# Graph-attention layer with a leading-row search on one Trainium2 core: another load order, another drain, and stores of one block

## The chip, the cores and the metric

The kernel runs on one core of one Trainium2 chip. A core has five engines, each with an instruction stream of its own, which it works off in order: TensorE (PE in the profile; its weight loads are PEld), VectorE (DVE), ScalarE (ACT), GpSimd (POOL) and SyncE (SP). Here SP only issues DMAs, GpSimd issues the indirect ones, and ScalarE issues a few. Matmuls write PSUM, the other engines work on PSUM and SBUF, and 16 DMA engines move data between SBUF and HBM. The metric is the device time of one execution in microseconds (us), lower is better.

## The reference

One graph-attention layer with a residual and a layer norm. x is 4096 x 512, adj is 4096 x 4096 and stands for additive masks, W is 512 x 2048 (four heads of 512), all float32:

```python
ht = (h @ W).reshape(N, N_HEADS, N_HIDDEN).transpose(1, 0, 2)
src = jnp.einsum('hnd,hd->hn', ht, a_src)
dst = jnp.einsum('hnd,hd->hn', ht, a_dst)
e = jax.nn.leaky_relu(src[:, :, None] + dst[:, None, :], SLOPE) + adj_mat[None]
att = jax.nn.softmax(e, axis=-1)
h_prime = jnp.einsum('hij,hjd->hid', att, ht)
return h_prime.mean(axis=0)
...
x = _layernorm(x + _L0_gnn_ref(x, adj, L0_gnn_W, L0_gnn_a), axis=-1)
```

The entries of adj reach 1e9, so in nearly every row one entry leads the others by so much that the softmax is 1 at that column and 0 elsewhere, for every head. Then the layer's output in that row is the row of x at the leading column, times the mean of the four heads of W.

## The kernel before, in words

`leading_rows` (line 66) computes every row that way and also tests whether that was allowed; `general` (line 389) computes the full attention for the row blocks where it was not. The test's result is one number, `any_bad`, which the engines load at line 60 to skip `general`; with these inputs it is skipped.

The 4096 rows are 32 blocks of 128, one row to a partition, and row p of block ib is row 32p + ib of the matrix. Per block:

- `load_adj` (101) brings 128 x 4096 numbers of adj, 2 MB, in one DMA on the SP queue (four DMAs for the first and the last block). There are six buffers, and a load is issued five blocks ahead.
- `segment_maxima` (146): VectorE takes the largest of each of 64 segments of 64 numbers, in two reductions of half a row (four pieces for the first and last block). `find_segment` (159) takes the eight largest segment maxima (`top`) and their places, and GpSimd gathers the leading segment of each row again from HBM (`lead`, 256 B a row).
- `find_column` (173), two blocks later: the largest in the segment (`inner`), its place, and so the column; GpSimd then gathers that row of x (`y`, 2 KB a row).
- `project` (189), three blocks later: TensorE turns y by four transposes into PSUM (`tp`, line 201), ScalarE copies that to SBUF (`yt`, line 203), and TensorE adds in PSUM the residual, as a matmul of the block of x with the identity (line 194), and four matmuls of yt with `w_sum`, the mean of the heads (line 209). A float32 matmul shows in the trace as two instructions.
- `stats` (215), `rstd` (222) and `finish` (227): mean and variance on ScalarE, the square root on ScalarE with a reciprocal and a product on VectorE, for two blocks at a time, and the normalised block written by ScalarE into `hold`. `hold` has a place of 512 numbers per partition for each of the 32 blocks. It first holds x, and W in places 16 to 31, and at the end the output.

W comes as four blocks of 1 MB (`load_w`, 111), and x as eight groups of four blocks (`load_x`, 108). `mean_of_heads` (245) adds the four heads of one W block on TensorE. `turn_w` and `head_vector` turn W for the vectors that the test's bound needs, spread over t = 1 to 14, and `bound` runs at t = 28 to 30.

The order of the work is written out by hand: each engine runs its instructions in the order in which the program names them. The loop at line 334 runs t over the 32 blocks. In the order of lines 335 to 366 it issues loads, half of the maxima of block t, the column of block t - 2, the other half, the segment of block t, the projection of block t - 3, statistics of block t - 4, and every second t the finishes of blocks t - 6 and t - 5.

The drain starts at line 368 when the loop is over: columns of blocks 30 and 31, finishes of 26 and 27, stores of blocks 0 to 27 in seven DMAs of four blocks (8 KB in a run), the test (309), whose count over the partitions is a small matmul (320) and three small operations of VectorE, and then projections of 29, 30 and 31, each followed by statistics and finish of the block before it. `finish_last` (231) normalises block 31 on VectorE with its batch-norm instructions, and ScalarE's queue stores it.

A DMA on the SP queue waits on SP for its buffer or its data, and everything behind it on that queue waits too.

Of the kernel before, what the change touches and what calls it, by code (L numbers as in the profile page):

```python
# [9 lines left out]
F32 = mybir.dt.float32  # L10
U32 = mybir.dt.uint32
# [8 lines left out]
P = 128  # L20
# [45 lines left out]
def leading_rows(ctx, tc, x, adj, W, a, out, ident, v, n_bad, any_bad):  # L66
# [7 lines left out]
    nc = tc.nc  # L74
# [4 lines left out]
    Q = 4  # L79
# [31 lines left out]
    def load_w(kb):  # L111
        nc.sync.dma_start(hold[:, ds(w_at + kb * H, H), :], w_blocks[:, kb])

    load_adj(0)
    for s in range(2):
        nc.scalar.dma_start(a_rows[ts(s, H), :], a[:, ts(s, D), :].rearrange("h d o -> h (d o)"))
    load_w(0)
    load_w(1)
    load_adj(1)
    load_w(2)  # L120
    load_w(3)
    load_adj(2)
    load_x(0)
    for ib in range(3, AHEAD):
        load_adj(ib)

    make_identity(nc, ident)
# [15 lines left out]

    seg_of, at_of, lead_of, y_t, o_ps = {}, {}, {}, {}, {}

    def segment_maxima(ib, part):

        if part == 0:
            seg_of[ib] = small.tile([P, S], F32, name="seg")
        n = PIECES if ib in (0, NB - 1) else 2  # L150
        for k in range(part * n // 2, (part + 1) * n // 2):
            nc.vector.tensor_reduce(  # L152
                seg_of[ib][:, ts(k, S // n)],
                adj_t[ib][:, ts(k, N // n)].rearrange("p (s e) -> p s e", e=E), axis=AX.X, op=OP.max,
            )
        if part == 1:
            del adj_t[ib]

    def find_segment(ib):
        seg = seg_of.pop(ib)  # L160
# [9 lines left out]
        )  # L170
        at_of[ib], lead_of[ib] = at, lead

    def find_column(ib):
        lead = lead_of.pop(ib)
        nc.vector.max(out=inner[:, ib, :], in_=lead)  # L175
        within = small.tile([P, 8], U32, name="within")
        nc.vector.max_index(within, inner[:, ib, :], lead)  # L177
        col = small.tile([P, 1], U32, name="col")
        nc.vector.scalar_tensor_tensor(  # L179
            col, at_of.pop(ib)[:, 0:1], float(E), within[:, 0:1], op0=OP.mult, op1=OP.add  # L180
        )
        y = rows.tile([P, D], F32, name="y", bufs=4)
        nc.gpsimd.indirect_dma_start(  # L183
            out=y, out_offset=None, in_=x,
            in_offset=bass.IndirectOffsetOnAxis(ap=col[:, :1], axis=0),
        )
        y_t[ib] = y

    def project(ib, between=(), wait=False):

        o = o_ps[ib] = psum.tile([P, D], F32, name="o")

        def residual():
            nc.tensor.matmul(o, ident, hold[:, ib, :], start=True, stop=False)  # L194

        if wait:
            residual()
        y = y_t.pop(ib)
        tp = psum.tile([P, KB, P], F32, name="tp", bufs=2)
        for kb in range(KB):  # L200
            nc.tensor.transpose(tp[:, kb, :], y[:, ts(kb, P)], ident)  # L201
        yt = rows.tile([P, KB, P], F32, name="yt")
        nc.scalar.copy(yt, tp)  # L203
        if not wait:
            residual()
        for some in between:
            head_vector(*some)
        for kb in range(KB):
            nc.tensor.matmul(o, yt[:, kb, :], w_sum[:, kb, :], start=False, stop=(kb == KB - 1))  # L209

    def row_norm(ib):
        sq = rows.tile([P, D], F32, name="sq")
# [15 lines left out]
        i = slice(ib, ib + 1)  # L228
        nc.scalar.activation(hold[:, ib, :], o_ps.pop(ib), AF.Identity, bias=nm[:, i], scale=sd[:, i])  # L229

    def finish_last(ib):
        o = o_ps.pop(ib)
        st = small.tile([P, nc.vector.BN_STATS_DIM], F32, name="st", bufs=1)
        nc.vector.bn_stats(st, o)
        mv = small.tile([P, nc.vector.BN_AGGR_DIM], F32, name="mv", bufs=1)
        nc.vector.bn_aggr(mv, st)
        r = small.tile([P, 1], F32, name="r", bufs=1)
        nc.scalar.activation(r, mv[:, 1:2], AF.Sqrt, bias=eps)
        nc.vector.reciprocal(r, r)
        nc.vector.tensor_scalar(hold[:, ib, :], o, mv[:, 0:1], r, op0=OP.subtract, op1=OP.mult)  # L240
# [52 lines left out]
    def bound(part):  # L293
# [11 lines left out]
        else:  # L305
            nc.vector.tensor_mul(lead_by, of_bound[1], vn)
            nc.vector.tensor_scalar(lead_by, lead_by, 1.05, 110.0, op0=OP.mult, op1=OP.add)

    def test():
        a1 = top[:, :, 0]  # L310
        gap = once.tile([P, NB], F32, name="gap")
        nc.vector.tensor_tensor(gap, top[:, :, 1], inner[:, :, 1], op=OP.max)
        size = once.tile([P, NB], F32, name="size")
        nc.vector.scalar_tensor_tensor(size, a1, -1.0, a1, op0=OP.mult, op1=OP.max)
        nc.vector.tensor_sub(gap, a1, gap)
        nc.vector.tensor_scalar(size, size, -(2.0 ** -22), lead_by, op0=OP.mult, op1=OP.subtract)
        nc.vector.scalar_tensor_tensor(gap, gap, 0.9999, size, op0=OP.mult, op1=OP.add)
        nc.vector.tensor_scalar(gap, gap, 0.0, None, op0=OP.is_gt)
        pg = psum.tile([1, NB], F32, name="px", bufs=1)
        nc.tensor.matmul(pg, ones[:, 0:1], gap, start=True, stop=True)  # L320
        nc.vector.tensor_scalar(n_bad, pg, -1.0, float(P), op0=OP.mult, op1=OP.add)
        total = once.tile([1, 1], F32, name="total")
        nc.vector.tensor_reduce(total, pg, axis=AX.X, op=OP.add)
        nc.vector.tensor_scalar(any_bad, total, -1.0, float(N), op0=OP.mult, op1=OP.add)
# [9 lines left out]
    for t in range(NB):  # L334
        if t in x_at:
            load_x(x_at[t])
        load_adj(t + AHEAD)
        segment_maxima(t, 0)
        if t >= COLUMN:
            find_column(t - COLUMN)  # L340
        segment_maxima(t, 1)
        find_segment(t)
        pair = t >= FINISH and t % 2 == 0
        if pair:
            rstd(slice(t - FINISH, t - FINISH + 2))
        if t == 0:
            for kb in range(KB):
                mean_of_heads(kb)
            turn_a()
        turned = [(*vectors[0], turn_w(*vectors.pop(0))) for _ in range(vectors_at.get(t, 0))]  # L350
        if t == 16:
            head_norms()
        if 28 <= t <= 30:
            bound(t - 28)
        if t >= PROJECT:
            project(t - PROJECT, turned)
        else:
            for some in turned:
                head_vector(*some)
        if pair:  # L360
            finish(t - FINISH)
            finish(t - FINISH + 1)
        if t >= STATS:
            stats(t - STATS)
        for ib in norms_at.get(t, ()):
            row_norm(ib)

    find_column(NB - 2)
    find_column(NB - 1)
    rstd(slice(NB - FINISH, NB - FINISH + 2))  # L370
    finish(NB - FINISH)
    finish(NB - FINISH + 1)
    for g in range(NB // Q - 1):
        store(nc.sync, g * Q, Q)
    test()
    for ib in range(NB - PROJECT, NB):
        project(ib, wait=(ib == NB - 1))
        stats(ib - 1)
        rstd(slice(ib - 1, ib))
        finish(ib - 1)  # L380
        if ib == NB - 2:
            store(nc.sync, NB - Q, 2)
    store(nc.sync, NB - 2, 1)
    finish_last(NB - 1)
    store(nc.scalar, NB - 1, 1)


# [232 lines left out]
```

## Time and profile before

| what | value |
|---|---|
| time, median of 6 runs | 256.96 us (256.31 to 258.1) |
| the profiled execution | 258.13 us, of which the span of the program's instructions is 256.4 us |
| busy share of the span | TensorE 80%, VectorE 75%, ScalarE 47%, GpSimd 24% |
| moved by DMA | 97.75 MB, mean 381 GB/s |
| VectorE's reductions (line 152) | 68, 146.2 us busy |
| TensorE's matmuls with w_sum (line 209) | 256, 119.6 us busy, 610 ns mean |
| TensorE's residuals (line 194) | 64, 36.3 us busy, 652 ns mean |
| adjacency loads, 2 MB each | 32.6 us from issue to landing (median) |
| gathers of x | 8.2 us from issue to landing (median) |
| stores of four blocks, 1 MB each | 25.9 us from issue to landing (median) |

The page of the profile shows one execution. Its rows of digits cut the span into 40 slices of 6.4 us, where a digit is the busy share in tenths (PEclk is the clock granted to TensorE, in tenths of full speed). A line of the timeline gives start and duration in us, the engine, the line of the program and the operation, then output and inputs by the program's names, and in brackets how long the engine had been idle and what released it. A "q" behind an engine's name is its instruction sequencer, which issues DMAs.

### The profile page before, as it was taken

How to read it: one execution, taken by the hardware profiler on the slowest of the kernel's cores; microseconds unless marked ns; L12 is line 12 of the kernel's file. 1: busy time of each engine (PE TensorE's matmuls, PEld its weight loads, DVE VectorE, ACT ScalarE, POOL GpSimd, SP SyncE). 2: the span in 40 equal slices, each digit the busy share in tenths (PEclk: the TensorE clock that was granted, in tenths of full speed). 3: DMA queues.
4: the chain of work that ended last, by engine and by line, in shares of the span. 5: the costliest groups of instructions: out<-in, count | busy, mean ns of one | idle time of the engine just before them, and what ended most of it. 6: DMA issues, size and time to landing. Idle time of an engine off the chain costs nothing.

```text
span 256.4 us, 2438 instructions
## 1 busy us (share of the span) xinstructions
PE 205.8 (80%) x683; PEld 104.9 (41%) x684; DVE 191.9 (75%) x381; ACT 120.3 (47%) x295; POOL 61.8 (24%) x75
## 2 busy tenths in 40 slices
PE   0099995999898999998595978888785989929960
PEld 0033584655554556653242424333332434404420
DVE  3508379969979997997989999999799999721011
ACT  2000322357645475755272537575655555615450
POOL 1100022222222322232212332323223222310000
PEclk9999965999999999999999799999999799986997
DMA  7999999999999999999999999999999999975021
GB/s 247 410 422 435 422 425 422 414 424 430 418 421 421 422 427 419 425 414 422 424 422 422 422 419 420 423 432 417 417 421 428 414 404 425 426 299 206 35 91 50
DMA packets 12259, 97.75 MB, mean 381 GB/s; under 512 B 1992, under 2 KB 1992, under 8 KB 5968
## 3 DMA queue, kind: packets, MB, share of 16 engines
q1 hardware_dynamic: 8496, 87.82, 82.0%
q0 software_dynamic: 3584, 9.44, 9.5%
q10 hardware_dynamic: 160, 0.28, 0.3%
q8 instruction: 7, 0.11, 0.2%
q14 instruction: 12, 0.10, 0.1%
HBM read 89.15 MB, written 8.39 MB: 380 GB/s over the span
## 4 chain that ended last, share of the span: by engine, by line
DMA 59%; DVE 27%; PE 9%; issue 2%; ACT 0%; POOLq 0%; SPq 0%
DMA adj_t<-in_adj_dram 41%; DVE seg L152 20%; DMA hold<-in_L_gnn_W_dram 7%; PE o L209 6%; DMA y<-in_x_dram,col 6%; DMA lead<-in_adj_dram,row 6%; PE o L194 2%; DVE within L177 1%; DVE at L163 1%; PE tp L201 1%; DVE top L161 1%; DVE inner L175 1%; DVE col L179 1%; DVE row L165 1%; DVE hold L240 0%
## 5 line engine op out<-in xcount | busy, mean ns | idle before, releaser
L152 DVE TENSOR_REDUCE seg<-adj_t 128x32 f32<-128x2048 f32 (+1 forms) x68 | 146.2, 2154 | 28.9 <-DMA adj_t<-in_adj_dram 28.8
L209 PE MATMUL o<-w_sum,yt 128*128 128x512 f32 x256 | 119.6, 610 | 0.7 <-ACT yt L203 0.7
L209 PEld LDWEIGHTS o<-w_sum,yt 128*128 128x128 f32 x256 | 47.5, 195 | 61.5 <-issue 48.7
L183 POOL DMA_INDIRECT y<-in_x_dram,col x32 | 30.2, 945 | 97.9 <-issue 79.8
L167 POOL DMA_INDIRECT lead<-in_adj_dram,row x32 | 30.3, 948 | 70.7 <-DVE row L165 47.4
L203 ACT COPY yt<-tp 128x512 f32<-128x512 f32 x32 | 18.8, 586 | 52.0 <-PE tp L201 43.0
L201 PE MATMUL tp<-ident,y 128*128 128x128 f32 x128 | 21.3, 292 | 20.1 <-DMA y<-in_x_dram,col 20.1
L194 PE MATMUL o<-hold,ident 128*128 128x512 f32 x64 | 36.3, 652 | 0.0
L201 PEld LDWEIGHTS tp<-ident,y 128*128 128x128 f32 x128 | 15.0, 148 | 33.2 <-issue 30.6
L248 PE MATMUL o<-hold,ident 128*128 128x512 f32 x32 | 16.7, 682 | 12.6 <-DMA hold<-in_L_gnn_W_dram 12.6
L229 ACT ACTIVATE hold<-o,nm,sd 128x512 f32<-128x512 f32 x31 | 22.6, 779 | 7.9 <-DVE nm L225 7.9
L266 ACT COPY wt<-tp 128x512 f32<-128x512 f32 x16 | 9.2, 586 | 33.2 <-PE tp L264 30.1
L220 ACT ACTIVATE sq<-o,nm 128x512 f32<-128x512 f32 x31 | 21.3, 687 | 1.0
L272 PEld LDWEIGHTS pv<-at_d,wt 128*128 128x128 f32 x128 | 18.3, 212 | 7.2 <-issue 4.6
L213 ACT ACTIVATE sq<-hold 128x512 f32<-128x512 f32 x32 | 19.8, 619 | 0.0
L218 ACT ACTIVATE sq<-o 128x512 f32<-128x512 f32 x31 | 18.7, 604 | 0.0
L272 PE MATMUL pv<-at_d,wt 128*128 128x2 f32 x128 | 17.1, 258 | 0.5 <-ACT wt L266 0.5
L248 PEld LDWEIGHTS o<-hold,ident 128*128 128x128 f32 x32 | 6.8, 220 | 21.4 <-issue 20.2
L249 ACT ACTIVATE w_sum<-o 128x512 f32<-128x512 f32 x4 | 2.4, 597 | 24.6 <-PE o L248 24.6
L224 DVE RECIPROCAL sd<-sd 128x2 f32<-128x2 f32 (+1 forms) x17 | 2.7, 159 | 14.6 <-ACT sd L223 14.6
L175 DVE MAX8 inner<-lead 128x8 f32<-128x64 f32 x32 | 7.0, 218 | 5.8 <-DMA lead<-in_adj_dram,row 5.8
L194 PEld LDWEIGHTS o<-hold,ident 128*128 128x128 f32 x64 | 10.6, 207 | 0.5 <-issue 0.5
(66 smaller groups left out, 94.8 us busy)
## 6 DMA issues: line engine op xcount, KB each, us to landing
adj_t<-in_adj_dram SPq DMA_DIRECT2D x30, 2048.0 KB, 32.6
hold<-in_x_dram SPq DMA_DIRECT2D x8, 1024.0 KB, 29.5
out_dram<-hold SPq DMA_DIRECT2D x7, 1024.0 KB, 25.9
adj_t<-in_adj_dram SPq DMA_DIRECT2D x8, 512.0 KB, 6.7
hold<-in_L_gnn_W_dram SPq DMA_DIRECT2D x4, 1024.0 KB
lead<-in_adj_dram,row POOLq DMA_INDIRECT x32
y<-in_x_dram,col POOLq DMA_INDIRECT x32, 8.2
out_dram<-hold SPq DMA_DIRECT2D x1, 512.0 KB
```

Of the source, the lines that this page charges most:

```text
L152: nc.vector.tensor_reduce(seg_of[ib][:, ts(k, S // n)], adj_t[ib][:, ts(k, N // n)].rearrange("p (s e) -> p s e", e=E), axis=AX.X, op=OP.max,)
L167: nc.gpsimd.indirect_dma_start(out=lead, out_offset=None, in_=adj_segs, in_offset=bass.IndirectOffsetOnAxis(ap=row[:, :1], axis=0),)
L183: nc.gpsimd.indirect_dma_start(out=y, out_offset=None, in_=x, in_offset=bass.IndirectOffsetOnAxis(ap=col[:, :1], axis=0),)
L194: nc.tensor.matmul(o, ident, hold[:, ib, :], start=True, stop=False)
L201: nc.tensor.transpose(tp[:, kb, :], y[:, ts(kb, P)], ident)
L203: nc.scalar.copy(yt, tp)
L209: nc.tensor.matmul(o, yt[:, kb, :], w_sum[:, kb, :], start=False, stop=(kb == KB - 1))
L213: nc.scalar.activation(sq, hold[:, ib, :], AF.Square, accum_out=xx[:, ib : ib + 1])
L220: nc.scalar.activation(sq, o, AF.Square, bias=nm[:, i], accum_out=sd[:, i])
L229: nc.scalar.activation(hold[:, ib, :], o_ps.pop(ib), AF.Identity, bias=nm[:, i], scale=sd[:, i])
L248: nc.tensor.matmul(o, ident, hold[:, w_at + kb * H + h, :], start=(h == 0), stop=(h == H - 1))
L272: nc.tensor.matmul(pv[:, kb, h : 2 * H : H], wt[:, k, :], at_d[:, k, h : 2 * H : H], start=(k == 0), stop=(k == KB - 1),)
```

## The change

Four things change, and all the other lines stay.

- **Loads.** Before: adj 0, W 0, W 1, adj 1, W 2, W 3, adj 2, x 0, adj 3, adj 4. After: adj 0, W 0, adj 1, W 1, adj 2, W 2, adj 3, W 3, adj 4, x 0. The means of heads follow: block 0 at t = 0, 1 at t = 1, 2 and 3 at t = 2 (before, all four at t = 0).
- **Block 31's maxima.** At t = 31 only the first of four pieces stands ahead of `find_column(29)`, the other three behind it.
- **Drain.** For block 31 the column comes from a search of the whole row of 4096 for its largest value, without the gathered segment; the segment is still gathered, and its `inner` is taken later, for the test. The test is cut in two, and its matmul and three small operations come behind the projection of block 30. Blocks 29 and 30 no longer add the residual on TensorE: `finish_last` adds it on VectorE and normalises these blocks there. Block 31's copy from PSUM is shared by ScalarE and VectorE.
- **Stores.** Blocks 0 to 23 go out in 24 DMAs of one block, with 2 KB in a run, ahead of the finishes of 26 and 27 in program order; then 24 to 27 in one, and 28 to 31 each in one.

```diff
-    load_w(0)
-    load_w(1)
-    load_adj(1)
-    load_w(2)
-    load_w(3)
-    load_adj(2)
+    for kb in range(KB):
+        load_w(kb)
+        load_adj(kb + 1)
     load_x(0)
...
+    def find_inner(ib):
+        nc.vector.max(out=inner[:, ib, :], in_=lead_of[ib])
+
+    def find_column_in_row(ib):
+
+        col = small.tile([P, 8], U32, name="col")
+        nc.vector.max_index(col, top[:, ib, :], adj_t[ib])
+        gather_rows(ib, col)
...
-        nc.scalar.copy(yt, tp)
-        if not wait:
+        if order == "residual turn":
+            half = KB // 2
+            nc.scalar.copy(yt[:, :half, :], tp[:, :half, :])
+            nc.vector.tensor_copy(yt[:, half:, :], tp[:, half:, :])
+        else:
+            nc.scalar.copy(yt, tp)
+        if order == "turn residual":
             residual()
...
-    def finish_last(ib):
+    def finish_last(ib, residual):
+
         o = o_ps.pop(ib)
+        if residual:
+            nc.vector.tensor_add(hold[:, ib, :], o, hold[:, ib, :])
+            o = hold[:, ib, :]
...
     find_column(NB - 2)
-    find_column(NB - 1)
+    find_column_in_row(NB - 1)
     rstd(slice(NB - FINISH, NB - FINISH + 2))
+    for ib in range(NB - 2 * Q):
+        store(nc.sync, ib, 1)
     finish(NB - FINISH)
     finish(NB - FINISH + 1)
-    for g in range(NB // Q - 1):
-        store(nc.sync, g * Q, Q)
+    store(nc.sync, NB - 2 * Q, Q)
+    project(NB - 3, order="turn")
+    find_inner(NB - 1)
     test()
-    for ib in range(NB - PROJECT, NB):
-        project(ib, wait=(ib == NB - 1))
-        stats(ib - 1)
-        rstd(slice(ib - 1, ib))
-        finish(ib - 1)
-        if ib == NB - 2:
-            store(nc.sync, NB - Q, 2)
+    stats(NB - 4)
+    rstd(slice(NB - 4, NB - 3))
+    finish(NB - 4)
+    store(nc.sync, NB - 4, 1)
+    finish_last(NB - 3, True)
+    store(nc.sync, NB - 3, 1)
+    project(NB - 2, order="turn")
+    count()
+    finish_last(NB - 2, True)
     store(nc.sync, NB - 2, 1)
-    finish_last(NB - 1)
+    project(NB - 1, order="residual turn")
+    finish_last(NB - 1, False)
     store(nc.scalar, NB - 1, 1)
```

## The prediction

> **What bounds the kernel now.** I read the forty slices first, then the chain of waits, then the timeline of the last 50 us, and last the stretches of the clock.
>
> ```profile
> PE   0099995999898999998595978888785989929960
> DVE  3508379969979997997989999999799999721011
> PEclk9999965999999999999999799999999799986997
> DMA  7999999999999999999999999999999999975021
> GB/s 247 410 422 435 422 425 422 414 424 430 418 421 421 422 427 419 425 414 422 424 422 422 422 419 420 423 432 417 417 421 428 414 404 425 426 299 206 35 91 50
> ```
>
> A slice is 6.4 us. Up to slice 35 (228 us) the DMA engines are full at 404 to 435 GB/s: 97.75 MB at 422 GB/s are 232 us of the 256.4 us span. Nothing before 228 us can gain unless bytes go, and none go. What can move is the drain, the last 28 us, where the GB/s row falls away. There the timeline shows what ends last:
>
> ```profile
> 228.60 0.23 DVE L175 MAX8 inner<-lead 128x8 f32<-128x64 f32 x1 [5.45 <-DMA lead<-in_adj_dram,row]
> 229.66 1.45 ACT L229 ACTIVATE hold<-o,nm,sd 128x512 f32<-128x512 f32 x2 [5.80 <-DVE nm L225]
> 230.65 0.27 PE L320 MATMUL px<-gap,ones 128*1 128x32 f32 x2 [4.77 <-DVE gap L318]
> 233.46 4.75 PE L209 MATMUL o<-w_sum,yt 128*128 128x512 f32 x8
> 239.34 3.68 PE L209 MATMUL o<-w_sum,yt 128*128 128x512 f32 x8
> 244.99 1.55 PE L209 MATMUL o<-w_sum,yt 128*128 128x512 f32 x3 [0.68 <-ACT yt L203]
> 248.73 0.70 DVE L234 BATCH_NORM_STATS2 st<-o 128x6 f32<-128x512 f32 x1 [1.67 <-PE o L209]
> 249.46 0.18 DVE L236 BATCH_NORM_AGGREGATE mv<-st 128x2 f32<-128x6 f32 x1
> 249.68 0.29 ACT L238 ACTIVATE r<-mv,eps 128x1 f32<-128x1 f32 x1 [1.81 <-DVE mv L236]
> 250.21 0.81 DVE L240 TENSOR_SCALAR hold<-o,mv,r 128x512 f32<-128x512 f32 x1
> 251.05 0.39 ACTq L243 DMA_DIRECT2D out_dram<-hold  x1
> ```
>
> (Columns: start, duration, engine, line, operation; in brackets the idle time and its releaser.) VectorE waits 5.45 us for the last gathered segment. The count of the test (L320) stands ahead of block 29's projection on TensorE, so TensorE idles 4.77 us, then runs blocks 29, 30 and 31 with almost no hole until 248.73. From there 2.32 us lead to the last store, and 5.28 us (251.05 to 256.33) to the end. The idle time has a second price:
>
> ```profile
> 136.78:140.19 3.41, 1.31 (x4) 0.24 (x2) 3.33 (x6) 0.00 (x0) 0.94 (x1) 1.00 1.01 429
> 140.19:143.60 3.41, 2.77 (x7) 1.74 (x8) 3.25 (x9) 1.64 (x3) 0.94 (x1) 0.50 1.02 424
> 225.53:228.94 3.41, 0.35 (x1) 0.00 (x0) 0.31 (x3) 0.00 (x0) 0.00 (x0) 1.00 0.89 369
> 228.94:232.35 3.41, 1.70 (x7) 1.33 (x8) 1.93 (x14) 1.80 (x3) 0.94 (x1) 0.50 0.26 66
> 232.35:235.76 3.41, 3.41 (x5) 1.32 (x4) 0.32 (x2) 2.67 (x7) 0.00 (x0) 0.50 0.90 362
> ```
>
> (Stretch, length, then busy us of TensorE, its weight load, VectorE, ScalarE, GpSimd, then the granted clock, DMA share, GB/s.) After a stretch with 0.35 us of TensorE work the clock is halved for two stretches. Block 29 from its transposes (230.84) to block 30's takes 7.2 us, where block 30 takes 238.04 to 242.86 = 4.8: the half clock cost 2.4 us. Without it this span would have been 254.0.
>
> **The start.** The order of the loads changes, not their bytes. Block 1 comes one W block (1.05 MB, 2.5 us at 422 GB/s) earlier, block 2 two (5 us), and the last W block later by some 10 us. VectorE starts sooner, but the DMA row is full anyway: worth 0. Against it, TensorE gets two means of heads later. At 125 us a gather waited 4.1 us for TensorE, and the rate between 120 and 128 us was still 419 GB/s, since adjacency loads are issued 32.6 us ahead. So the loss too is 0; I allow 0.5 us each way.
>
> **The stores.** 6.3 MB go out as 24 stores in 2 KB runs instead of six in 8 KB. In the trace a 2 KB packet holds a DMA engine 86 ns, an 8 KB one 309 ns, so 3072 packets on 16 engines take 16.5 us, not 14.8: 1.7 us more, ending near 230. On SP 24 issues of 0.33 us are 8 us of a queue that has nothing else from 191.36 on; stores 24 to 27 stand behind them but wait for ScalarE's finish anyway (229.5), and nobody waits for a store before the end. Worth 0. A gather of x (four 4 KB packets an engine, 160 ns each, in turn with store packets) lands 4 x (309 - 86) = 0.9 us sooner; it gains only where a gather is late, and below none is. The Trainium skill, "DMA: Bandwidth & Descriptors", section "Bandwidth", asks for batches of 1 MiB and speaks against 256 KB stores (it measured 138 GB/s at 64 KB, 341 at 1 MB). An estimate from that page, at some 250 GB/s, would put their end at 238 us, still ahead of the final store. No run here shows such a loss; the 86 ns row gives 381 GB/s.
>
> **The search.** Block 31's segments end at 221.7 as now, since the four reductions and one column search are only reordered (block 29's gather goes 1.2 us sooner). Row and top 222.5, block 30's column 223.15. Then VectorE scans 4096 elements. No row shows that. The 64-wide search takes 0.22; the reductions give 2280 - 1215 = 1065 ns for 1024 more elements, 1.04 ns each; so 0.22 + 4032 x 1.04 ns = 4.4 us. The ends are 0.22 (width free) and 8.6 (two passes); I take 4.4, as one value a step is what the nearest wide row does. It ends at 227.7, against 229.35 now: 1.7 us gained. The gather of x behind it lands by 234 and is not needed before 240.
>
> **The queue behind it.** This search now stands ahead of the reciprocal and product for blocks 26 and 27 (0.3 us, to 228.0), which ScalarE's two finishes await (1.45 us, to 229.4), and behind those stands block 29's copy (0.58). TensorE, no longer blocked by the count, turns block 29 once its gather lands (issued at 219.0, 6.8 to 8.2 us on its way, so 226 to 228), and then idles until the copy is there. Its matmuls thus start at 230.0 instead of 233.46.
>
> **The chain from block to block.** Here I see the loss. The finish of 29 is written ahead of 30's projection, so ScalarE's square root for 29 stands ahead of 30's copy. After 29's last matmul come: add of 128x512, not shown (between 0.6, 512 elements at 1.04 ns plus some 0.1, and 0.81, L240; I take 0.70, L234), statistics 0.70, aggregate 0.18, root 0.29, steps between them 0.13: 2.0 us. Then 30's copy, 0.58 + 0.07. TensorE waits 2.65 us where now it had 1.1 us of transposes and residual to do and no hole. After 30's matmuls the count comes in as well (L320 to L324: 230.65 to 231.40, 0.75), then 2.0, then half a copy (0.4; it was 0.58): 3.2 us. The residual of 31 and its transposes (1.3 us) lie beside that.
>
> **The sum at full clock.** 230.0 + 3.7 = 233.7; + 2.65 + 3.7 = 240.05; + 3.2 + 3.7 = 246.95; + 2.32 + 5.28 = 254.55. The profiled run at full clock was 254.0: there block 29's matmuls would start at 232.2, and 14.2 us (one block of 4.8, and 239.34 to 248.73) lie from there to the last matmul, against 16.95 now. So 2.2 us are gained at the front, 2.75 spent on the two waits, and 0.55 lost.
>
> **The clock.** The hole before block 29, 226 to 230 but for its transposes, is nearly as long as now (4.77), so one stretch at half clock is to be expected: 3.4 to 5 us of it, costing 1.7 to 2.5; I take 2.1. Span 256.65, with the 1.73 us that lie around the profiled span (258.13 - 256.4) 258.4. That execution was 1.2 above the median, 256.96; on the median's footing this is 257.2, and 258.4 on its own. I state 257.8, between, because the new waits give the clock two more occasions to fall. The Trainium skill, "TensorE: Matmul & The Clock Gate", section "Why this matters for your kernels", allows holes of up to about 3 us. By that rule the hole of 2.65 us is harmless and the sum stays. The rows above disagree: 1.31 us busy of 3.41, a total idle of 2.1, was enough at 140.19.
>
> **Rivals.** (1) Forecast: the waits behind the finishes eat the gain, clock lost once; 256.6 to 259.2; chance 0.54. (2) Faster: the clock holds, or the search is quicker than 4.4 us. For it: the hole is a microsecond or two shorter. At full clock 254.55 + 1.73 = 256.3, less the 1.2 by which the profile stood over the median, 255.1; with half the search (2.2 us less) and the clock lost once, 257.2 - 2.2 = 255.0. It decides if matmuls of block 29 start before 229 or run in 3.7 us; 0.22. (3) The clock falls a second time, in the waits of 2.65 and 3.2 us: 3.4 us at half clock cost 1.7 more: 259.5 (up to 261); 0.16. (4) The change doesn't do what it says: the small stores delay the gathers, segment 30 reaches VectorE after 222.5 (it had 0.6 us of slack), and everything shifts by as much, 1 to 3 us: 258.8 to 260.8; 0.08.
>
> Measurement tells 0.3% (0.77 us) from no change. Faster than 256.2: rival 2 and a little of 1, 0.22. Within: the low part of 1, 0.27. Slower than 257.7: 0.51. The range takes in most of 2, all of 1 and part of 3 and 4: 255.2 to 260.3.
>
> **What would show it.** Right: DMA full until 229; a search of 4.4 us ending near 227.7; block 29's transposes near 226 and its matmuls near 230; ScalarE's copy of block 30 released by the root, and TensorE idle some 2.6 and 3.2 us between the last three blocks; last matmul at 247 to 250. Wrong: a search far from 4.4 us, copies not held by the root, matmuls of 29 starting with its transposes, or VectorE waiting on a segment at 222.

## The result, and the profile after

The changed kernel takes 260.21 us in the median of 20 runs (258.09 to 261.88), the kernel before 257.23 us in 46 runs beside it (256.01 to 258.18): a ratio of 1.0111, with an interval of 1.0091 to 1.013. It is slower by 1.1%, some 3 us. The forecast was 257.8 within 255.2 to 260.3, slower with a chance of 0.51. So the side held, the range held by 0.09 us, and the likeliest case of it (256.6 to 259.2) did not: 6 of the 20 runs lie in it and 13 at 259.5 or above. A second series of the same kernel, in the first experiment, has a median of 259.28 us, so a difference from the changed kernel is given below as two numbers where the two medians make it differ. A ratio leaves out runs more than 1.5% above the fastest of their kernel, which touches one experiment alone (the start and the stores as before, three runs of twelve).

The profiled execution, 258.1 us with a span of 256.3, is as short as the fastest of the 20; a longer one, 0.8 us above the median, is shown by the first experiment. First three rows of the forty slices of the changed kernel (6.4 us each):

```profile
PE   0279868999999999989498879698785989938760
...
PEclk9999798699999999999979999979999799997996
...
GB/s 253 435 417 435 405 421 424 413 423 426 415 414 417 422 414 418 418 414 419 421 413 423 418 416 414 414 417 418 422 422 410 419 396 400 390 374 330 41 43 50
```

The row of GB/s was to be as before up to slice 35. It is not quite: from the tenth slice on most read 413 to 422 where before they read 417 to 428. That small loss comes back below. The drain in the timeline (columns as before):

```profile
223.83 4.42 DVE L191 FIND_INDEX8 col<-top,adj_t 128x8 uint32<-128x4096 f32 x1
225.95 0.60 PE L206 MATMUL tp<-ident,y 128*128 128x128 f32 x4
228.54 1.45 ACT L242 ACTIVATE hold<-o,nm,sd 128x512 f32<-128x512 f32 x2 [4.45 <-DVE nm L238]
229.88 0.58 ACT L213 COPY yt<-tp 128x512 f32<-128x512 f32 x1
...
237.62 0.29 ACT L255 ACTIVATE r<-mv,eps 128x1 f32<-128x1 f32 x1 [4.23 <-DVE mv L253]
237.82 0.57 ACT L213 COPY yt<-tp 128x512 f32<-128x512 f32 x1
238.44 3.70 PE L219 MATMUL o<-w_sum,yt 128*128 128x512 f32 x8 [2.09 <-ACT yt L213]
244.56 0.35 ACT L210 COPY yt<-tp 128x256 f32<-128x256 f32 x1
244.97 3.70 PE L219 MATMUL o<-w_sum,yt 128*128 128x512 f32 x8 [1.18 <-ACT yt L210]
```

Block 29's transposes are done at 226.55, but its matmuls start at 230.52, because the copy of 229.88 stands behind the finishes of 26 and 27 (228.54), and these behind the search. Block 30's copy (237.82) comes right after the root of block 29's finish (237.62), as the prediction read from the order. The brackets show 2.09 and 1.18 us of idle TensorE. With block 30's transposes (0.6) before the one, and the count, residual and transposes of block 31 before the other, the waits from the last matmul of a block to the first of the next are 2.52 and 2.83 us. In the chain of work that ended last, block 29's matmuls stand as one piece:

```profile
230.52 5.41 PE o L219 x8
```

A block takes 3.7 us at full clock. The clock of the stretches says why this one took 5.41 (stretch, length, busy us of TensorE, its weight load, VectorE, ScalarE, GpSimd, granted clock, DMA share, GB/s):

```profile
227.39:230.80 3.41, 0.28 (x1) 0.29 (x2) 2.43 (x10) 2.26 (x4) 0.95 (x1) 1.00 1.01 374
230.80:234.22 3.42, 3.42 (x5) 1.36 (x5) 0.32 (x2) 2.10 (x6) 0.00 (x0) 0.50 1.03 393
234.22:237.63 3.41, 2.13 (x8) 0.88 (x6) 1.57 (x3) 0.01 (x1) 0.00 (x0) 1.00 0.53 215
```

After a stretch with 0.28 us of matmuls, one stretch at half clock costs 1.7 us. In this execution the wait before block 30 does not lower it again. That is luck: in the first experiment the same wait does.

### The profile page after: what moved, and what is told of

The parts are those of the page before. It is cut to its first block, busy times and chain, and to the rows that moved or that the text cites. A ratio compares the mean times of both kernels' runs of the same rounds, so it can differ in the third digit from the quotient of the medians.

```text
span 256.3 us, 2464 instructions
## 1 busy us (share of the span) xinstructions
PE 205.6 (80%) x679; PEld 104.7 (41%) x680; DVE 200.4 (78%) x387; ACT 114.7 (45%) x285; POOL 62.0 (24%) x75
## 4 chain that ended last, share of the span: by engine, by line
DMA 59%; DVE 27%; PE 5%; issue 4%; ACT 1%; SPq 1%; POOLq 0%
DMA adj_t<-in_adj_dram 55%; DVE seg L149 18%; PE o L219 5%; DMA y<-in_x_dram,col 4%; DVE col L191 2%; DVE within L181 1%; DVE at L158 1%; DVE top L156 1%; DVE st L251 1%; DVE col L183 1%; DVE inner L176 1%; ACT hold L242 1%; DVE row L160 1%; DVE hold L248 1%; SPq L106 1%
## 5 line engine op out<-in xcount | busy, mean ns | idle before, releaser
L219 PE MATMUL o<-w_sum,yt 128*128 128x512 f32 x256 | 123.0, 625 | 7.2 <-ACT yt L213 6.1
L219 PEld LDWEIGHTS o<-w_sum,yt 128*128 128x128 f32 x256 | 48.7, 200 | 68.9 <-issue 50.2
L199 PE MATMUL o<-hold,ident 128*128 128x512 f32 x60 | 33.7, 646 | 0.8 <-DMA hold<-in_x_dram 0.8
L265 PE MATMUL o<-hold,ident 128*128 128x512 f32 x32 | 18.4, 727 | 16.4 <-DMA hold<-in_L_gnn_W_dram 16.4
L242 ACT ACTIVATE hold<-o,nm,sd 128x512 f32<-128x512 f32 x29 | 21.2, 784 | 5.3 <-DVE nm L238 5.3
L233 ACT ACTIVATE sq<-o,nm 128x512 f32<-128x512 f32 x29 | 19.9, 687 | 0.9
L289 PEld LDWEIGHTS pv<-at_d,wt 128*128 128x128 f32 x128 | 17.2, 200 | 7.4 <-ACT wt L283 4.0
L231 ACT ACTIVATE sq<-o 128x512 f32<-128x512 f32 x29 | 17.6, 607 | 0.0
L289 PE MATMUL pv<-at_d,wt 128*128 128x2 f32 x128 | 16.0, 249 | 0.6 <-ACT wt L283 0.6
L281 PEld LDWEIGHTS tp<-ident,hold 128*128 128x128 f32 x64 | 7.9, 142 | 6.9 <-issue 6.9
L281 PE MATMUL tp<-ident,hold 128*128 128x128 f32 x64 | 9.3, 273 | 0.0
```

The lines of the kernel that those rows point to most:

```text
L219: nc.tensor.matmul(o, yt[:, kb, :], w_sum[:, kb, :], start=(kb == 0 and order == "turn"), stop=(kb == KB - 1),)
L233: nc.scalar.activation(sq, o, AF.Square, bias=nm[:, i], accum_out=sd[:, i])
L265: nc.tensor.matmul(o, ident, hold[:, w_at + kb * H + h, :], start=(h == 0), stop=(h == H - 1))
L289: nc.tensor.matmul(pv[:, kb, h : 2 * H : H], wt[:, k, :], at_d[:, k, h : 2 * H : H], start=(k == 0), stop=(k == KB - 1),)
```

## The experiments

The theory (A): the order of the drain makes the copies of blocks 29, 30 and 31 wait for ScalarE and VectorE; that costs half a microsecond at full clock, and the rest of the loss is the clock, which falls once in the wait before block 29 and in most executions again in the wait before block 30. The rivals: (B) the new order of loads and the small stores cost it, by later gathers; (C) the added work on VectorE, or TensorE's share of the work, sets the end; (D) the test's wait for the last segment was the true bound of the kernel before, so that moving the count alone would have brought all of the gain.

### The changed kernel again

Nothing is edited.

> The changed kernel once more, for a second profile and more times. Theory A (the three last blocks run one after the other through VectorE's statistics and ScalarE's root, and the holes this leaves on TensorE let the clock fall a second time in most executions): times spread again over 258 to 262 us with a median near 260.2; a profile whose execution lies near the median shows the clock at 0.5 once more after the first drop, in or behind the holes ahead of the matmuls of blocks 30 or 31, and its last matmul 1.5 to 3.5 us later than 248.7. Rival B (the small stores or the start of the loads cost it, before the drain): the last reduction of block 31 or the whole-row search ends later than 228.3 in such an execution, and the clock is as in the first profile.

Measured: 259.28 us (258.63 to 261.35, 9 runs), ratio 1.0092 (1.0056 to 1.0129). Six of the times lie at 258.6 to 260 and three at about 261, but the 20 runs of the result fill the gap between (260.06 to 260.86), so it is a spread and not two groups. The profiled execution is one of the long ones, 260.98 us with a span of 259.2. Its blocks 29 and 30 in the timeline:

```profile
230.71 6.47 PE L219 MATMUL o<-w_sum,yt 128*128 128x512 f32 x8 [3.89 <-ACT yt L213]
239.71 5.39 PE L219 MATMUL o<-w_sum,yt 128*128 128x512 f32 x8 [2.09 <-ACT yt L213]
```

and its stretches:

```profile
226.10:229.51 3.41, 0.72 (x5) 0.42 (x4) 2.79 (x4) 0.77 (x2) 0.31 (x1) 1.00 1.04 391
229.51:232.92 3.41, 2.21 (x3) 1.17 (x4) 1.34 (x8) 2.92 (x9) 0.64 (x1) 0.50 1.01 354
232.92:236.33 3.41, 3.41 (x5) 1.35 (x4) 0.00 (x0) 0.67 (x1) 0.00 (x0) 0.50 0.85 349
236.33:239.75 3.42, 1.33 (x7) 0.54 (x5) 2.06 (x5) 0.77 (x2) 0.00 (x0) 1.00 0.01 3
239.75:243.16 3.41, 3.41 (x4) 1.48 (x5) 0.22 (x1) 0.00 (x0) 0.00 (x0) 0.50 0.20 77
```

Here is the second fall: 1.33 us of matmuls in the stretch 236.33 to 239.75, and block 30 then runs at half clock (5.39 us where 3.7 would do). The first is also longer here: the stretch that begins at 229.51 has only 2.21 us of matmuls in it, since block 29 starts in its middle, and the next one stays at half clock. Blocks 29 and 30 together lose 2.77 + 1.69 = 4.5 us, where the prediction allowed 2.1. Where the stretches' bounds fall against the waits differs from one execution to the next, and the time with it. The profiles of all the runs here together say how empty a stretch has to be: after the first 60 us, every stretch at full clock with 1.35 us of matmuls or less was followed by one at half clock, every one with 1.51 us or more was not, and between the two both occur. This holds for that part of the kernel. Before 60 us, where W is turned and many matmuls write two numbers a row, stretches with 2.6 to 3.2 us busy were followed by half clock too.

### Idle matmuls in the three waits

```diff
+    def keep_warm(n):
+        pw = psum.tile([P, D], F32, name="px", bufs=1)
+        for _ in range(n):
+            nc.tensor.matmul(pw, ident, w_sum[:, 0, :], start=True, stop=True)
...
+        if warm:
+            keep_warm(warm)
         for kb in range(KB):
             nc.tensor.matmul(
```

Behind the transposes of blocks 29, 30 and 31 stand 4, 2 and 1 matmuls that nobody reads. It adds work and shortens no wait of the chain.

> The changed kernel with idle matmuls (the identity times the mean of the heads, into a PSUM bank that nobody reads) in the three holes of TensorE: four ahead of block 29's matmuls, two ahead of 30's, one ahead of 31's, each 0.86 us at full clock. They add work and no wait. Theory A: the clock stays at 1.0 to the end, the sum at full clock holds: last matmul at 247.0, span 254.6, time 256.4 us, and the spread shrinks from 3.8 us to about 1. Theory A without the clock (the holes alone cost it, the spread is something else): 260 us, unchanged. Rival B: 260 us, unchanged.

Measured: 257.03 us (256.56 to 257.88, 12 runs), ratio 0.9985 (0.9965 to 1.0006), no difference from the kernel before that can be told. Blocks 29, 30 and 31 in the timeline:

```profile
230.76 3.70 PE L226 MATMUL o<-w_sum,yt 128*128 128x512 f32 x8 [0.53 <-ACT yt L218]
...
236.99 3.70 PE L226 MATMUL o<-w_sum,yt 128*128 128x512 f32 x8 [0.38 <-ACT yt L218]
...
243.51 3.70 PE L226 MATMUL o<-w_sum,yt 128*128 128x512 f32 x8 [0.32 <-ACT yt L215]
```

The stretches beside them (columns as before) are fuller, and the clock stays at 1.00:

```profile
227.02:230.44 3.42, 3.21 (x8) 1.14 (x6) 3.04 (x10) 1.66 (x3) 0.95 (x1) 1.00 1.03 378
230.44:233.85 3.41, 3.09 (x7) 1.44 (x8) 0.32 (x2) 2.70 (x7) 0.00 (x0) 1.00 1.03 366
233.85:237.27 3.42, 3.04 (x11) 1.43 (x10) 2.28 (x5) 0.77 (x2) 0.00 (x0) 1.00 0.59 240
```

Blocks 30 and 31 start 2.53 and 2.82 us after the block before has ended, as in the changed kernel, and each block takes 3.70. The last matmul ends at 247.21; the prediction's sum at full clock had 246.95. More work on TensorE, and 3.2 us off the median of 260.21 (2.3 us off the 259.28 of the same series): that is what the clock costs the changed kernel. The spans agree: 259.2 less 254.8 is 4.4, and the first experiment's execution lost 4.5 in its two blocks.

### Idle matmuls in the two later waits only

As the last one, with 0, 2 and 1 of them.

> The changed kernel with the idle matmuls in the two later holes alone (two ahead of block 30's matmuls, one ahead of 31's), so that the first hole stays empty. Theory A: the first drop of the clock stays (3.4 to 6.8 us at 0.5 from about 230 on, 1.7 to 2.9 us lost), a second one behind 236 does not come: median 258.5 to 259.2 us, none over 260. Without theory A's second drop: as the changed kernel, median 259.3 to 261 with times over 261.

Measured: 258.79 us (258.28 to 260.96, 7 runs), ratio 1.0085 (1.0048 to 1.0121). Four runs lie at 258.3 to 258.8, and three at 260.3 to 261.0, where none over 260 was expected. In the profiled execution (258.28) block 29 takes 5.15 us, and block 30 a full-clock 3.70. So the first fall is there and the second is not. Two fillers take 1.88 us at full clock in the profile; at half clock they would take about twice that, 3.8 us (an estimate), and outlast the wait. That could make the three slow runs, but no profile of such a run was taken, so it stays argued.

### The projections ahead of the finishes

```diff
+    project(NB - 2, order="turn")
     finish_last(NB - 3, True)
     store(nc.sync, NB - 3, 1)
-    project(NB - 2, order="turn")
     count()
+    project(NB - 1, order="residual turn")
     finish_last(NB - 2, True)
     store(nc.sync, NB - 2, 1)
-    project(NB - 1, order="residual turn")
     finish_last(NB - 1, False)
```

Only the order is changed: block 30's copy no longer stands behind the root of 29's finish, nor 31's behind that of 30's.

> The changed kernel with the order of four steps turned: block 30's projection is named ahead of block 29's finish, and 31's ahead of 30's, with the count behind 29's finish. No work is added or taken. Theory A: TensorE's waits of 2.65 and 3.2 us shrink to 1.1 and some 2.0 (with 1.6 us of work in them), so 2.85 us less at full clock, and the clock falls once only: span about 254, time 255.5 to 256.5 us. Rival B: 260 us less nothing but what TensorE saves in the drain if it were the bound, so 259 to 260.

Measured: 256.6 us (255.96 to 257.92, 12 runs), ratio 0.9979 (0.9953 to 1.0005), 0.1 us above what was expected. The last three blocks:

```profile
230.98 6.45 PE L219 MATMUL o<-w_sum,yt 128*128 128x512 f32 x8 [3.97 <-ACT yt L213]
...
238.54 3.70 PE L219 MATMUL o<-w_sum,yt 128*128 128x512 f32 x8 [0.68 <-ACT yt L213]
...
244.34 3.70 PE L219 MATMUL o<-w_sum,yt 128*128 128x512 f32 x8 [0.46 <-ACT yt L210]
```

Block 29's matmuls are slow, but those of 30 and 31 run at full clock: the waits are 1.1 and 2.1 us instead of 2.5 and 2.8, and the second fall is gone. Two projections moved in the program take 3.6 us off the changed kernel's median (2.7 us off that of the same series).

### The residuals back on TensorE

```diff
-    project(NB - 3, order="turn")
+    project(NB - 3)
...
-    finish_last(NB - 3, True)
+    finish_last(NB - 3, False)
```

The same for block 30. TensorE gets one matmul a block more (two instructions in the trace, 1.02 us), VectorE an addition of 0.69 us less.

> The changed kernel with the residuals of blocks 29 and 30 on TensorE again, behind the transposes, and so without VectorE's addition; the order of the steps stays. Theory A: the addition (0.7 us) leaves the chain from block to block twice and the residual (0.86 us) lies in the hole: 1.4 us less at full clock, and the second drop is rarer: median 257 to 258.5 us. Rival (TensorE's work is what counts, so the residuals on VectorE are the useful part): 1.7 us slower than the changed kernel, 261 to 262.

Measured: 257.5 us (255.13 to 258.12, 12 runs), ratio 0.9994 (0.9968 to 1.0021). The work that the change took off TensorE is back and the kernel is 2.7 us faster than the changed one (1.8 us by its second series). Two of its blocks:

```profile
231.28 5.40 PE L219 MATMUL o<-w_sum,yt 128*128 128x512 f32 x8 [3.09 <-ACT yt L213]
...
238.49 3.70 PE L219 MATMUL o<-w_sum,yt 128*128 128x512 f32 x8 [0.51 <-ACT yt L213]
```

Block 30's matmuls begin 1.8 us after block 29's end (238.49 behind 236.68), its residual lies in that time, and in the profile only block 29 is slow. The two waits are 1.81 and 2.10 us, 1.4 us shorter together than in the changed kernel, since VectorE's addition is out of them; what is left of the gain, 0.4 to 1.3 us, fits a clock that falls once and not twice. Rival C is out as to TensorE's work: what counts is what fills the wait and how long it is.

### The start and the stores as before, in the changed drain

```diff
-    for kb in range(KB):
-        load_w(kb)
-        load_adj(kb + 1)
+    load_w(0)
+    load_w(1)
+    load_adj(1)
+    load_w(2)
+    load_w(3)
+    load_adj(2)
...
-    for ib in range(NB - 2 * Q):
-        store(nc.sync, ib, 1)
+    for g in range(NB // Q - 2):
+        store(nc.sync, g * Q, Q)
```

All four means of heads are again at t = 0.

> The changed kernel with two of its four parts undone: the loads of W and adj and the means of heads in the order of before, and the stores of blocks 0 to 23 in six DMAs of four blocks. The drain stays as changed. Theory A: 260.2 us, within 0.5, since neither part has anything waiting for it. Rival B: back to 257.2 us.

Measured: 258.44 us (256.47 to 262.26, 12 runs), ratio 1.0016 (0.9981 to 1.005) from the nine runs under 260.5; the mean of all twelve, 259.08, is 0.6% above the kernel before. The median is 1.8 us under the 260.2 that was expected, but only 0.8 under the changed kernel's 259.28 in the same series, and with times spread over nearly 6 us that difference can't be told from none. In the profile (260.22) block 29 is turned at 227.34 instead of 225.95, since its gather lands later. The bracket of idle TensorE ahead of its matmuls is then 2.79 us instead of 3.96, and both blocks 29 and 30 take 5.40.

### The stores alone as before

> The changed kernel with the stores of blocks 0 to 23 in six DMAs of four blocks, as before, and nothing else undone. In the run that undid the start as well, block 29's gather landed 1.1 us later, so TensorE turned that block at 227.3 and not at 226.0, and its hole ahead of the matmuls was 2.9 us, not 4.0. Theory A with the clock: the hole is shorter, the clock drops less often, so the times reach down to 256.5 and the median is 1 to 2 us under the 259.3 to 260.2 of the changed kernel, with the transposes of block 29 at about 227.3. Rival (the start of the loads is what mattered there): median 259.5 to 260.5 and none under 258.

Measured: 261.31 us (258.55 to 261.83, 6 runs), ratio 1.0128 (1.0085 to 1.0172). It was expected to be a microsecond or two below the changed kernel and lies above. Block 29 is turned at 227.55, its matmuls take 6.68 us and block 30's 5.40: the first fall held for two stretches, as in the first experiment. So the two runs that undo the stores differ by 2.9 us with the same drain, and in both the clock falls twice. With six and twelve runs of a time that hangs on where the stretches fall, they cannot say what the start or the stores are worth. The next run says it for the two together.

### The start and the stores as before, with the clock held

The edit of the start and the stores, and 3, 2 and 1 idle matmuls.

> The changed kernel with idle matmuls in all three holes (three in the first, which is shorter here), and the start of the loads and the stores as before the change. The clock holds, so what these two parts cost in the changed drain shows without it. Theory A: the time of the run with idle matmuls and both parts, 257.0 us, within 0.5, since block 29's copy waits for ScalarE either way. Rival B: 1 us or more below 257.0.

Measured: 256.93 us (256.25 to 257.63, 12 runs), ratio 0.9984 (0.9967 to 1.0001), against 257.03 with the new start and the small stores and the clock held. With the clock out of it, the two edits together are worth nothing in this drain. Rival B is out.

### The same operations in another order

```diff
     find_column(NB - 2)
-    find_column_in_row(NB - 1)
     rstd(slice(NB - FINISH, NB - FINISH + 2))
+    find_column_in_row(NB - 1)
...
     project(NB - 3, order="turn")
-    find_inner(NB - 1)
-    test()
     stats(NB - 4)
     rstd(slice(NB - 4, NB - 3))
     finish(NB - 4)
     store(nc.sync, NB - 4, 1)
+    project(NB - 2, order="turn")
+    find_inner(NB - 1)
+    test()
     finish_last(NB - 3, True)
     store(nc.sync, NB - 3, 1)
-    project(NB - 2, order="turn")
     count()
+    project(NB - 1, order="residual turn")
     finish_last(NB - 2, True)
     store(nc.sync, NB - 2, 1)
-    project(NB - 1, order="residual turn")
```

All of the change is kept, and no operation is added or taken away. The small reciprocal and product for blocks 26 and 27 stand ahead of the long search, the projections ahead of the finishes, and the test behind block 30's projection.

> The changed kernel with the drain's steps in another order and no work added or taken: reciprocal and product for blocks 26 and 27 ahead of the whole-row search, block 30's projection ahead of block 29's finish, 31's ahead of 30's. Theory A: block 29's matmuls start with its copy at 227.2, the last three blocks follow each other with 1.1 and 1.9 us between, no hole is over 2 us, the clock holds: last matmul at 241.2, span 249, time 250.5 to 252 us. Rival B (it is not the order but the drain's work): no more than the 256.6 us of the run that turned the projections alone.

Measured: 251.84 us (251.04 to 253.2, 6 runs), ratio 0.9784 (0.975 to 0.9817): 2.2% faster than the kernel before, and 8.4 us below the changed one (7.4 by its second series). The timeline:

```profile
225.39 4.42 DVE L191 FIND_INDEX8 col<-top,adj_t 128x8 uint32<-128x4096 f32 x1
225.44 1.45 ACT L242 ACTIVATE hold<-o,nm,sd 128x512 f32<-128x512 f32 x2 [0.43 <-DVE sd L237]
...
228.14 3.70 PE L219 MATMUL o<-w_sum,yt 128*128 128x512 f32 x8 [0.68 <-ACT yt L213]
...
233.04 3.70 PE L219 MATMUL o<-w_sum,yt 128*128 128x512 f32 x8 [0.67 <-ACT yt L213]
...
238.84 3.70 PE L219 MATMUL o<-w_sum,yt 128*128 128x512 f32 x8 [0.46 <-ACT yt L210]
```

The search begins 1.6 us later than in the changed kernel (0.9 of it because the last reduction ends later, at 223.31 and not 222.38) and costs nobody anything, because the finishes (225.44) run beside it. Block 29 starts at 228.14 instead of 230.52, the waits are 1.2 and 2.1 us, and the clock is 1.00 from 224.5 to 246.3, behind the last matmul. All the work that the change gave VectorE is still there, so rival C is out as a whole. What the change lost, it lost by the order of its instructions, and not for want of an engine's time.

### That order without the whole-row search

Block 31's column comes from the gathered segment, as in the kernel before: `find_column(NB - 1)` in place of `find_column_in_row(NB - 1)` and `find_inner(NB - 1)`.

> As the run with the new order, but block 31's column comes from the gathered segment again, as before the change, and not from the search of the whole row. Theory A: block 31's row of x arrives 1 to 1.5 us later, at about 234, and is not needed before 236.5, so the time is that of the run with the search, within 0.5 us. Rival C (the search is the part of the change that is worth something): 1 to 2 us slower than that run.

Measured: 251.48 us (251.3 to 251.6, 6 runs), ratio 0.9767 (0.974 to 0.9793), the fastest median of all. The search of 4.42 us is worth nothing in this order; block 31's matmuls end at 242.12 without it and at 242.54 with it. The row of x for block 31 is wanted last of all, and there is time to gather the segment first.

### That order with the start and the stores as before

> As the run with the new order, with the start of the loads and the stores of blocks 0 to 23 as before the change. Here TensorE waits for block 29's row of x and for nothing else, so a gather that lands 1.1 us later (8 KB runs beside it, not 2 KB) shows: block 29's transposes at 227.3 and not 226.1, time 1 us above the run with the new order, with the clock at 1.0 in both. If the small stores are worth nothing even so: the same time within 0.4 us.

Measured: 252.74 us (252.16 to 253.78, 6 runs), ratio 0.9809 (0.9781 to 0.9837), 0.9 us above the same order with the small stores; the intervals overlap, so six runs of each don't settle it. Block 29's transposes, here and then with the small stores:

```profile
228.43 0.63 PE L209 MATMUL tp<-ident,y 128*128 128x128 f32 x4 [0.28 <-DMA y<-in_x_dram,col]
...
226.87 0.60 PE L206 MATMUL tp<-ident,y 128*128 128x128 f32 x4
```

From the end of the last reduction to them are 4.57 us (223.86 to 228.43), with the small stores 3.56 (223.31 to 226.87). With the stores alone as before, in the changed drain, it is 4.70 (222.85 to 227.55), so this is the stores and not the start. The packets of the gather itself say the same: from the end of its issue to its last packet are 4.2 to 4.7 us in the eight profiles with small stores and 5.3 to 5.6 us in the six others. The gather that goes out into the queues' traffic lands about a microsecond sooner beside packets of 2 KB than beside packets of 8 KB. The prediction worked out 0.9 for this from the two packets' durations. In this order block 29 starts as soon as its row is there, so it can count; in the changed kernel's own drain block 29 waits for its copy anyway, and it does not.

### The kernel before, with the count moved

```diff
         finish(ib - 1)
         if ib == NB - 2:
+            count()
```

`test` is cut in two as in the change, and the count comes behind block 30's projection. All else is the kernel before.

> The kernel before, with the test's matmul and its three small operations behind block 30's projection and nothing else changed. The test no longer blocks TensorE, so block 29 is turned at about 227. Theory A: its copy on ScalarE still stands behind the finishes of blocks 26 and 27, which wait for the same gathered segment, so its matmuls start near 231.8 and not at 228, against 232.2 at full clock before: the time stays within 1 us of 257.3. Rival D (the test's wait was the bound): 4 us faster, 253 us.

Measured: 256.41 us (255.27 to 257.37, 12 runs), ratio 0.9953 (0.9929 to 0.9978): 0.8 to 1.1 us of gain, and not the 4 that rival D had. Its timeline:

```profile
226.85 0.63 PE L201 MATMUL tp<-ident,y 128*128 128x128 f32 x4 [1.59 <-DMA y<-in_x_dram,col]
228.99 1.45 ACT L229 ACTIVATE hold<-o,nm,sd 128x512 f32<-128x512 f32 x2 [5.75 <-DVE nm L225]
230.32 0.58 ACT L203 COPY yt<-tp 128x512 f32<-128x512 f32 x1
230.96 5.40 PE L209 MATMUL o<-w_sum,yt 128*128 128x512 f32 x8 [2.62 <-ACT yt L203]
```

TensorE is free to turn block 29 at 226.85, but the copy (230.32) stands behind ScalarE's two finishes, and those behind VectorE's wait for the last segment. The wait for the count covered another one of nearly the same length.

## Why the prediction was right, and where not

**The search: right.** 4.4 us were worked out from the slope of the reductions, and the row has 4.42. It ended at 228.25 and not 227.7, because the last reduction ended at 222.38 and not 221.7.

**The queue behind the search and block 29's start: right.** 229.4 was forecast for the finishes and 230.0 for the matmuls; the finishes ended at 229.99, the matmuls began at 230.52, and in the other executions with this order of the drain at 230.7 to 231.4.

**The chain between the blocks: right.** Waits of 2.65 and 3.2 us were forecast, and 2.52 and 2.83 measured. In the second, the count holds the addition back by 0.57 us only (block 30's matmuls end at 242.14, the addition starts at 242.71), where 0.75 was allowed for, and from the addition to the copy are 1.85 us (to 244.56), where 2.0 were.

**The sum at full clock: right in the profile, 0.75 us short in the median.** 246.95 for the last matmul, and 247.21 with the clock held by idle matmuls, although the last reduction ended 0.9 us later there (222.63). As a time the sum is 254.55 + 1.73 = 256.28; the run with the clock held has 256.56 in its profile and 257.03 in the median. From that sum the prediction took off up to 1.2 us, because the profiled execution of the kernel before lay that far above its median (all of it in its rival 2, half in the 257.8). No run shows such a deduction: with the clock held, the median lies above the profiled execution and not below.

**The clock: the step that was mis-sized.** The prediction lost the clock once, for 2.1 us, and priced a second fall as a rival with a chance of 0.16 (259.5 up to 261). In the profiled execution of the first experiment it lost 4.5 us in two blocks, and over the runs the clock's price is the 260.21 of the changed kernel less the 257.03 with the clock held, 3.2 us. With the 259.28 of the second series it is 2.3 us. The median of 260.21 lies in the rival's range and not in the forecast's. Of the 2.4 us between it and the 257.8, the clock is 1.1 (3.2 for 2.1), the sum 0.75, and the deduction 0.6. That it lies in the stated range at all, by 0.09 us, is luck in part. The row that the prediction itself showed, 1.31 us busy in 3.41 and then half clock, was the right one to go by: 1.33 us did it again (236.33), and 2.13 did not (234.22 in the changed kernel's profile). The wait of 2.65 us, with 0.6 us of transposes, can leave a stretch as empty as that, and the forecast should have counted that as likely. The Trainium skill, "TensorE: Matmul & The Clock Gate", section "Why this matters for your kernels", takes holes of up to about 3 us for harmless; the wait of 2.5 us between blocks 29 and 30 is shorter and halved the clock in the first experiment. The measurement decides.

**The stores: right in their worth.** Worth 0 in this drain, by the pair of runs with the clock held, and a microsecond sooner for the gather, as worked out. VectorE did not wait for block 30's segment (its maximum at 223.10 follows the instruction before it without a hole), so the rival of late gathers is out. The stores of blocks 0 to 23 ended at 232.9 and not near 230, but they also began later, and from first packet to last they took 21.1 us where the kernel before took 20.9: the 1.7 us more that were worked out from the packets do not show.

**The DMA full as before: wrong by 1%, with the cause open.** The start was priced at 0, with 0.5 us each way. From 60 to 185 us the stretches are, in the kernel before and in the changed one:

```profile
60.00:185.00 125.00, 108.21 (x384) 55.77 (x383) 113.89 (x220) 70.87 (x179) 37.66 (x40) 0.99 1.01 422
```

```profile
60.00:185.00 125.00, 111.52 (x389) 57.95 (x388) 113.97 (x220) 73.46 (x185) 36.92 (x39) 0.97 1.01 418
```

The last column is 422 GB/s against 418. All kernels made from the changed one have 418 in that stretch, those with the start and the stores as before too, and the kernel before with only its count moved has 422. From the 5th to the 88th MB the kernel before takes 196.7 us, with its count moved too, the others 198.3 to 198.5: 1.7 us. So it is neither the order of the loads nor the stores. In the trace the 16 KB packets within a microsecond of a gather take 621 ns in the median against 614 in the kernel before; away from gathers both take 614. Among what those kernels share is the second buffer of `st`, `mv` and `r`, which can move the tiles behind them in SBUF. Whether that is the cause wasn't tried.

**What makes up the 3 us.** Two profiled executions stand about equally far above their medians: the kernel before (258.13 us, 0.9 above 257.23) and the first experiment's (260.98, 0.8 above 260.21). Their spans are 256.4 and 259.2, 2.8 apart. At full clock the one was 254.0 by the prediction's count, the other is 254.8 by the profile with the idle matmuls. So 0.8 us are the order of the drain and the later stream (block 29 starts at 230.76 there instead of 230.0, and the waits are 0.5 shorter together than forecast), and the other 2.0 are the clock, which costs the one 2.4 and the other 4.4. Of 2.8 us of loss the forecast had the first part nearly whole (0.55), and none of the second.

## What to carry to other kernels

An engine works off its queue in the order of the program: behind a long or waiting instruction, look up every short one that others wait for, and move it ahead. Here this alone, with no operation taken away, turned 1.1% slower into 2.2% faster, while the search brought nothing there, the count moved alone brought 0.8 to 1.1 us, and the residuals moved to VectorE cost 1.8 to 2.7 us in the change's own order. Taking work off TensorE where it would otherwise wait can cost more than that work did: here a stretch of 3.41 us with less than some 1.4 us of matmuls was followed by one at half clock. And where the time of one kernel is spread over some microseconds, hold the clock with idle matmuls first, and then compare the other edits.

## What the runs showed of the hardware that was not expected

- A stretch of 3.41 us with 1.33 us of matmuls was followed by one at half clock, and a stretch at half clock with 2.21 us of them by another one at half clock; 2.13 us in a stretch at full clock kept it. Over all the profiles, after the first 60 us, 1.35 us or less at full clock always lost it and 1.51 us or more never did.
- A search over 4096 float32 numbers a partition takes 4.42 us. Against the 0.22 us of one over 64 that is 1.04 ns for each further number, the pace of a reduction.
- A gather issued into full queues was used a microsecond sooner beside stores in 2 KB packets than beside 8 KB ones (3.56 against 4.57 us from the last reduction), while the stores of blocks 0 to 23 took about as long in both (21.1 and 20.9 us in the two main profiles).
- The stream ran at 418 instead of 422 GB/s in all kernels made from the changed one, whatever their order of loads and stores.
